# Two attention layers on one core: q and k of a head pair by seven block products, one PSUM tile for the preparation, and a second partial sum of p

## The chip, the core and the metric

The kernel runs on one core of a Trainium2 chip. The core has five instruction queues that run side by side and wait for one another by semaphores: TensorE (PE in the profile; its weight loads are listed apart as PEld), VectorE (DVE), ScalarE (ACT), GpSimd (POOL) and SyncE (SP). Here POOL and SP mostly issue DMA transfers. Each queue works in the order in which its instructions were written. The metric is the device time of one execution in microseconds (us).

## The reference

The input x has 16 images of 256 channels with 32 x 32 = 1024 positions. Two layers of the same form, with weights of their own, are applied to each image. A layer normalises in 16 groups, projects to q, k and v, and attends with 4 heads of 64 channels, where a position term is added to the scores:

```python
q, k, v = proj(Wq, bq), proj(Wk, bk), proj(Wv, bv)      # 256 x 256 times 256 x 1024
sim  = einsum('bhdi,bhdj->bhij', q, k)
rel  = (rel_h + rel_w).reshape(heads, d, n)
qpos = einsum('hdi,bhdj->bhij', rel, q)
attn = softmax(sim + qpos, axis=-1)
out  = einsum('bhdn,bhmn->bhdm', v, attn)
x = x + conv(gn(x))                                     # layer 0, then layer 1
```

Everything is float32. The group normalisation subtracts the mean of a group of columns and divides by its standard deviation.

## The kernel before

**Units, pairs and blocks.** A unit is one image in one layer; there are 32 of them, in an order in which a layer-1 unit stands several units behind its layer-0 unit. A unit has two pairs of heads (`pr`), since two heads of 64 channels fill 128 partitions. A pair has two halves of 512 query columns. A block is one unit, one pair and one half, so a unit has four blocks, b = 0 to 3. Blocks b = 0 and 2 are called even here, b = 1 and 3 odd; n is the number of the block from the start, 0 to 127.

**One block.** It makes eight score tiles j = 0 to 7 of 128 x 1024 (128 keys, two heads, 512 queries). For each, VectorE first writes the position term into a PSUM tile (`seed`, L341), TensorE adds the product of q and k onto it (`scores`, L370), and ScalarE takes exp out of PSUM into a buffer p in SBUF (L391). Then `attend` (L406) multiplies v with the eight p into a PSUM tile po, in two stretches: `values_of_p(0)`, the first score of the next block, then `values_of_p(1)`. ScalarE copies po out (`take_out`, L472). The softmax denominators need the sum of the eight p: `add_up` (L394) adds p 0 to 6 on VectorE, a DMA issued by POOL adds p 7 onto the sum (`add_last`, L432), and further DMAs fold the 128 partitions of that sum together (`fold`, `stack_up`, `fold_again`, `fold_stack`, `spread_sums`), until VectorE takes reciprocals. `finish` multiplies the output by them and adds the residual.

**Matmuls.** Nearly all are 64x64 tiles, four of which run in the array at the same time (two row halves, two column halves). `stretches` (L157) splits work that adds from both row halves into one PSUM bank into two stretches, the second of which waits for the end of the first.

**Preparation.** q, k, v and the position table of the next pair are made in between. `prepare` (L590) gives each block two pieces: b = 0: v of the second key half and q of pair 1; b = 1: k of pair 1 and its positions; b = 2 and 3: the same for pair 0 of the next unit. q and k of a pair (`project`, L255) are each two block products of 128 x 128 weights for each of the two column halves, so eight block products a pair. ScalarE takes each result out in one instruction (L276).

**PSUM.** PSUM holds four tiles of 128 x 1024, tags a to d, that go round in `ring`. In the kernel before, `f0, f1, f2, f3 = ring`; scores go through f0, f1 and f2, but f2 also takes one of the two preparation pieces, and f3 takes the other piece and then po.

**Normalisation.** ScalarE sums, squares and applies it group by group; `norms(u, b, i)` (L624) places these instructions at four places i of a block by tables. The reciprocal root comes from POOL (`rstd`, `nshift`, L234 and L236), between VectorE's reduction of the variance (L232) and ScalarE's applying (L245).

**What sets the order.** The whole fast path is written under a manual schedule: on each engine the instructions stand in the order in which `block` (L637) calls the functions, with nothing moved. The last two blocks of the last unit go through `block_without_pieces`; a general path behind a flag is not run on these inputs.

Of the kernel before, what the change touches and what calls it, by code (L numbers as in the profile page):

```python
# [9 lines left out]
F32 = mybir.dt.float32  # L10
# [7 lines left out]
P = 128  # L18
HALF = 512
G = 16  # L20
# [5 lines left out]
DEN_HI = 1e24  # L26

# [25 lines left out]
def fast_path(ctx, tc, sh, x, layers, out, W, den_all, good, flag):  # L53
# [38 lines left out]
    vpool = ctx.enter_context(tc.tile_pool(name="vpool", bufs=2))  # L92
    ppool = ctx.enter_context(tc.tile_pool(name="ppool", bufs=12))
    apool = ctx.enter_context(tc.tile_pool(name="apool", bufs=3))
# [38 lines left out]

    def taken(parts):
        for l, part in parts:
            w = {"Wq": W.wq, "Wk": W.wk, "Wv": W.wv}[part][l]
            nc.scalar.copy(w.rearrange("p a c -> p (a c)"), raw_t.pop((l, part)))

# [116 lines left out]
    def project(u, pr, which, pk):  # L255

        l = units[u][1]
        w, bias = (W.wk, W.bk) if which == "k" else (W.wq, W.bq)

        def products(t):  # L260
            for cc in range(CC):
                for rs, nh in BANKS[t]:
                    for h, c in enumerate(QUARTERS):
# [3 lines left out]
                            w[l][rs, cc, c0 : c0 + D],  # L267
# [14 lines left out]

    def values(u, g, pv):
        l = units[u][1]
        if g == 0:
            vts[u] = vpool.tile([P, NT, C], F32, tag="v", name=f"v_{u}")
# [17 lines left out]
        def out_of_psum():  # L304
            nc.scalar.copy(
                vts[u][:, 4 * g : 4 * g + 4, :].rearrange("p (a b) c -> p a b c", a=2), pv
            )
# [85 lines left out]

    def add_up(blk, j):  # L394
        u, pr, half = blk
        if j == 0:
            return
        if j == 1:
            accs[blk] = apool.tile([P, 2, HALF], F32, tag="acc", name=f"acc_{u}_{pr}_{half}")
            nc.vector.tensor_tensor(accs[blk], probs[blk, 0], probs[blk, 1], ALU.add)  # L400
        else:
            nc.vector.tensor_tensor(accs[blk], accs[blk], probs[blk, j], ALU.add)  # L402

    QUART = HALF // 2

    def attend(blk, po):  # L406
# [3 lines left out]
        def products(t):  # L410
            for j in range(NT):
                p = probs[blk, j]
                for rs, a in BANKS[t]:
                    for h, c in enumerate(QUARTERS):
# [3 lines left out]
                            vts[u][rs, j, c0 : c0 + D],  # L418
                            p[rs, h, a * QUART : (a + 1) * QUART],
                            start=(t == 0 and j == 0),  # L420
# [11 lines left out]
    def add_last(blk):  # L432
        nc.gpsimd.dma_start(accs[blk], probs[blk, NT - 1], accum_op=ALU.add)  # L433
# [156 lines left out]
    def prepare(u, b):  # L590

        x, y = ring[3], ring[2]
        if b == 0:
            return (
                values(u, 1, psum2(x, f"pv_{u}_1")),
                project(u, 1, "q", psum2(y, f"pq_{u}_1")),
            )
        if b == 1:
            return (
                project(u, 1, "k", psum2(x, f"pk_{u}_1")),  # L600
                positions(u, 1, psum2(y, f"pa_{u}_1")),
            )
        u += 1
        if u == NU:
            return (nothing, nothing), (nothing, nothing)
        if b == 2:
            return (
                project(u, 0, "q", psum2(x, f"pq_{u}_0")),
                project(u, 0, "k", psum2(y, f"pk_{u}_0")),
            )  # L610
        return (
            values(u, 0, psum2(x, f"pv_{u}_0")),
            positions(u, 0, psum2(y, f"pa_{u}_0")),
        )


    APPLY = {0: (0, 1, 5, 9, 9), 1: (9, 9, 9, 11, G)}
    SUMS = {0: (0, 0, 0, 2, 9), 1: (9, 11, 12, G, G)}
    SQUARES = {2: (0, 0, 5, 11, G)}
# [17 lines left out]
    def block(n):  # L637
# [3 lines left out]

        stacked = blocks[n - 3][:2] if half == 1 and n > 2 else None
        summed = blocks[n - 4][:2] if half == 0 and n > 3 else None
        before = blocks[n - 5][:2] if half == 1 and n > 4 else None
        after = blocks[n + 1] if n + 1 < len(blocks) else None
        previous = blocks[n - 1] if n > 0 else None
        one, two = u + 1 < NU, u + 2 < NU

        pieces = u + 1 < NU or b < 2
        if u + 1 == NU and b == 1:  # L650
            widen(u, 1)
        f0, f1, f2, f3 = ring
        folded = n - 1 < FOLDED
        if not pieces:
            return block_without_pieces(n, half)

        if previous:
            if half == 0:
                add_up(previous, 5)
            add_up(previous, 6)  # L660
            if folded:
                add_last(previous)
            else:
                add_up(previous, 7)
        for j in range(1 if n > 0 else 2, 4):
            scores(blk, j)
        (first, first_out), (second, second_out) = prepare(u, b)
        first(0)
        norms(u, b, 0)
        if n == 1:  # L670
            reduced(2, 1)
            added(2)
        seed(blk, 4, f1)
        scores(blk, 4)
        add_up(blk, 1)
        norms(u, b, 1)
        second(0)
        if half == 1:
            second_out()
        if stacked:  # L680
            fold_stack(*stacked, D)
        if summed:
            fold_stack(*summed, R // 8)
            spread_sums(*summed)
        if previous and folded:
            fold(previous)
        if stacked:
            fold_stack(*stacked, R)
        first(1)
        first_out()  # L690
        seed(blk, 5, f0)
        scores(blk, 5)
        if previous and folded:
            stack_up(previous)
# [557 lines left out]
```

## Time and profile before

| | |
|---|---|
| time, median of 3 runs (lowest to highest) | 2531.15 us (2530.21 to 2531.23) |
| profiled execution, first to last instruction (span) | 2528.3 us |
| difference, what lies around the span | 2.85 us against the median |
| busy: VectorE / ScalarE / POOL | 2268.4 / 1948.1 / 815.8 us |
| mean granted TensorE clock | 0.998 |
| DMA queue of POOL (software), share of 16 engines | 31.2% |
| DMA queue of SP (hardware), share of 16 engines | 12.0% |

The profile comes from one execution, and gives its span but no time of its own beyond it; the 2.85 us around it are taken as the same after the change. Matmuls are pipelined and their ends are modelled, so a row of TensorE shows a busy time that overlaps the next row; the distance from one start to the next is what a group takes. In a row of the timeline stand the start and the duration in us, engine, line, operation, tile written and read, and the count of instructions merged. Each float32 matmul shows as two instructions. In brackets stands the idle time before and what ended it.

### The profile page before, as it was taken

Reading aid. Unit: us, or ns where it says so; the run is one execution under the profiler, and the core shown is the slowest. Engines: PE = TensorE matmul, PEld = TensorE weight load, DVE = VectorE, ACT = ScalarE, POOL = GpSimd, SP = SyncE. Lnnn points to the kernel's source line nnn. Section 1 sums busy time; section 2 is a strip of 40 time slices with the busy share of each in tenths; the row PEclk is TensorE's granted clock in tenths of the full one; section 3 lists DMA queues with packets and bytes.
Section 4 is the critical chain, followed back from the end, with each engine's and each line's share of the span. In section 5 each row is a group of like instructions: output and inputs, shape, how many; then the busy total and the mean of one; then the engine's idle time right before and its main releaser. Section 6 shows DMA issues by size and latency. Waiting matters only on the chain.

```text
span 2528.3 us, 85680 instructions
## 1 busy us (share of the span) xinstructions
PE 2507.9 (99%) x37472; PEld 1332.2 (53%) x37472; DVE 2268.4 (90%) x2143; ACT 1948.1 (77%) x3855; POOL 815.8 (32%) x876
## 2 busy tenths in 40 slices
PE   8999999999999999999999999999999999999998
PEld 4555555555555555555555555555555555555554
DVE  7898998999989989999899899998998999989998
ACT  6778777788777787777877778877778777787754
POOL 1332333323333333333233332333333333323320
PEclk9999999999999999999999999999999999999999
DMA  3344444454444444444444444444454444444442
GB/s 94 74 83 80 78 87 77 90 103 88 99 91 101 80 84 95 90 81 98 89 88 96 82 96 80 84 105 91 88 112 81 88 80 84 77 85 80 95 84 67
DMA packets 119838, 221.56 MB, mean 88 GB/s; under 512 B 53912, under 2 KB 55448, under 8 KB 119456
## 3 DMA queue, kind: packets, MB, share of 16 engines
q0 software_dynamic: 53712, 130.10, 31.2%
q1 hardware_dynamic: 65744, 85.90, 12.0%
q8 instruction: 296, 4.85, 0.8%
q14 instruction: 86, 0.70, 0.1%
HBM read 51.78 MB, written 17.30 MB: 27 GB/s over the span
## 4 chain that ended last, share of the span: by engine, by line
PE 96%; DVE 2%; DMA 1%; issue 0%; SPq 0%; ACT 0%; POOL 0%; DVEq 0%; ACTq 0%; POOLq 0%
PE po L416 34%; PE ps L382 34%; PE pv L295 9%; PE pq L265 9%; PE pk L265 8%; PE pa L323 2%; DVE ps L346 1%; DVE acc L402 1%; DMA den_all<-d 0%; PE pm L206 0%; DMA stack<-stack 0%; DMA stack<-acc 0%; DVE acc L400 0%; DMA acc<-p 0%; DMA x<-in_x_dram 0%
## 5 line engine op out<-in xcount | busy, mean ns | idle before, releaser
L346 DVE TENSOR_TENSOR ps<-abt 128x1024 f32<-128x1024 f32 x1018 | 1227.3, 1228 | 228.1 <-ACT p L391 142.9
L391 ACT ACTIVATE p<-ps,shift 128x1024 f32<-128x1024 f32 x1024 | 1092.0, 1115 | 331.8 <-PE ps L382 331.8
L382 PE MATMUL ps<-q,k 64*64 64x512 f32 x8192 | 985.9, 590 | 1.4 <-DVE ps L346 1.2
L416 PE MATMUL po<-p,v 64*64 64x256 f32 x16384 | 930.5, 376 | 0.0
L416 PEld LDWEIGHTS po<-p,v 64*64 64x64 f32 x16384 | 629.4, 133 | 363.4 <-issue 80.9
L402 DVE TENSOR_TENSOR acc<-acc,p 128x1024 f32<-128x1024 f32 x643 | 780.6, 1214 | 7.0
L382 PEld LDWEIGHTS ps<-q,k 64*64 64x64 f32 x8192 | 308.1, 133 | 396.4 <-issue 273.6
L462 POOL DMA_DIRECT2D stack<-stack x310 | 302.3, 975 | 241.9 <-DMA stack<-stack 203.3
L457 POOL DMA_DIRECT2D stack<-acc x248 | 212.9, 982 | 447.3 <-DMA stack<-acc 395.3
L438 POOL DMA_DIRECT2D acc<-acc x124 | 102.8, 829 | 517.1 <-DMA acc<-p 504.4
L433 POOL DMA_DIRECT2D acc<-p x124 | 114.7, 925 | 405.9 <-ACT od L477 254.6
L295 PE MATMUL pv<-Wv,xn 64*64 64x256 f32 x4096 | 244.2, 376 | 0.0
L265 PE MATMUL pk<-xn,Wk 64*64 64x512 f32 x2048 | 242.9, 589 | 0.0
L265 PE MATMUL pq<-xn,Wq 64*64 64x512 f32 x2048 | 242.8, 589 | 0.0
L245 ACT ACTIVATE xn<-x,nshift,rstd 128x128 f32<-128x128 f32 x496 | 211.2, 499 | 0.0
L295 PEld LDWEIGHTS pv<-Wv,xn 64*64 64x64 f32 x4096 | 153.8, 133 | 101.8 <-issue 52.7
L187 ACT ACTIVATE junk<-x,neg 128x128 f32<-128x128 f32 x505 | 197.8, 402 | 0.0
L477 ACT COPY od<-po 128x512 f32<-128x512 f32 x127 | 74.4, 586 | 116.5 <-PE po L416 116.5
L400 DVE TENSOR_TENSOR acc<-p,p 128x1024 f32<-128x1024 f32 x128 | 156.0, 1218 | 0.0
L265 PEld LDWEIGHTS pq<-xn,Wq 64*64 64x64 f32 x2048 | 78.2, 133 | 141.0 <-issue 132.4
L187 ACT ACTIVATE junk<-x 128x128 f32<-128x128 f32 x464 | 141.0, 314 | 0.0
L265 PEld LDWEIGHTS pk<-xn,Wk 64*64 64x64 f32 x2048 | 75.3, 133 | 123.2 <-issue 122.9
(77 smaller groups left out, 1044.8 us busy)
## 6 DMA issues: line engine op xcount, KB each, us to landing
acc<-p POOLq DMA_DIRECT2D x124, 512.0 KB, 5.5
rden<-rd SPq DMA_DIRECT2D x126, 256.0 KB, 6.1
acc<-acc POOLq DMA_DIRECT2D x124, 256.0 KB, 3.5
x<-in_x_dram SPq DMA_DIRECT2D x32, 512.0 KB, 4.0
stack<-acc SPq DMA_DIRECT2D x248, 64.0 KB, 2.1
stack<-acc POOLq DMA_DIRECT2D x248, 64.0 KB, 2.9
out_dram<-x SPq DMA_DIRECT2D x31, 512.0 KB, 3.7
stack<-stack POOLq DMA_DIRECT2D x62, 128.0 KB, 7.1
```

What stands on the lines that cost most here:

```text
L187: nc.scalar.activation(junk, grouped(xt[units[u][0]], g), func, accum_out=into[:, g : g + 1], **bias)
L245: nc.scalar.activation(grouped(xns[u], g), grouped(xt[units[u][0]], g), AF.Identity, bias=shift[:, g : g + 1], scale=rstd[:, g : g + 1],)
L265: yield nc.tensor.matmul(pk[c, nh, :], w[l][rs, cc, c0 : c0 + D], xns[u][rs, cc, nh * HALF : (nh + 1) * HALF], start=(t == 0 and cc == 0), ...
L295: yield nc.tensor.matmul(pv[c, a, i, :], xns[u][rs, cc, j0 : j0 + D], W.wv[l][rs, cc, :], start=(t == 0 and cc == 0 and i == 0), stop=(t = ...
L346: nc.vector.tensor_tensor(ps.rearrange("p h (w y) -> p h w y", y=H), ab[:, :, :H].unsqueeze(2).to_broadcast([P, 2, XH, H]), ab[:, :, H + h ...
L382: nc.tensor.matmul(ps[c, h, :], a[hs, j0 : j0 + D], b[hs, columns], start=bool(tag) and i == 0, stop=i == len(terms) - 1, skip_group_check ...
L391: nc.scalar.activation(p, ps, AF.Exp, bias=W.shift)
L400: nc.vector.tensor_tensor(accs[blk], probs[blk, 0], probs[blk, 1], ALU.add)
L402: nc.vector.tensor_tensor(accs[blk], accs[blk], probs[blk, j], ALU.add)
L416: yield nc.tensor.matmul(po[c, a, :QUART], vts[u][rs, j, c0 : c0 + D], p[rs, h, a * QUART : (a + 1) * QUART], start=(t == 0 and j == 0), s ...
L457: nc.gpsimd.dma_start(at, acc[R:D, h, :], accum_op=ALU.add)
L462: nc.gpsimd.dma_start(stack[:rows_], stack[rows_ : 2 * rows_], accum_op=ALU.add)
```

## The change

**Seven block products.** For a pair, the 2 x 2 block matrix of weights (rows q and k, columns the two channel chunks) meets the 2 x 2 block matrix of the normalised input (rows the chunks, columns the two halves). Before, eight block products are made. Now seven are made from sums and differences of blocks (the scheme of Strassen and Winograd). `forms` builds the sums of weights once per layer, in blocks 1 and 2 of the run; `input_sums` builds the four sums of inputs T1, T3, T2 and T4 on VectorE once per unit, in b = 2 of the unit before. Only the first unit's pairs keep the old way (`project`, called "plain").

```diff
+    def alone(u, pr, ps):
+        f = W.form[units[u][1]]
+        for h, c in enumerate(QUARTERS):
+            c0 = pr * P + h * D
+            nc.tensor.matmul(
+                ps[c, 0, :], f[:, A11, c0 : c0 + D], xb(u, 0, 0),
+                start=True, stop=True, skip_group_check=True,
+            )
+        nc.scalar.copy(ps[:, 1, :], ps[:, 0, :])
+    def two_products(u, pr, step, ps):
+        left, right = (
+            ((S2, A12), (ts[u][:, T2], xb(u, 1, 0))),
+            ((S1, S3), (ts[u][:, T1], ts[u][:, T3])),
+            ((S4, NA22), (xb(u, 1, 1), ts[u][:, T4])),
+        )[step]
...
+    def q_half(u, pr, nh, ps):
+        nc.scalar.activation(
+            qs[u, pr][:, nh * HALF : (nh + 1) * HALF], ps, AF.Identity,
+            bias=W.bq[units[u][1]][:, pr : pr + 1],
+        )
+    def keep(u, pr, nh, ps):
+        nc.scalar.copy(ks[u, pr][:, nh * HALF : (nh + 1) * HALF], ps[:, 0, :])
+    def k_half(u, pr, nh, ps):
+        k = ks[u, pr][:, nh * HALF : (nh + 1) * HALF]
+        nc.vector.scalar_tensor_tensor(
+            k, ps[:, 1, :], W.bk[units[u][1]][:, pr : pr + 1], k, ALU.add, ALU.add,
+        )
```

`alone` is the one product that is made by itself, from 128x64 tiles; ScalarE then copies its result beside it inside PSUM, since it goes into several sums. `two_products` makes two of the other six at a time, in two stretches of 64x64 tiles. Per pair ScalarE has that copy, two `keep` and two `q_half`, each 128 x 512, in place of two instructions of 128 x 1024; VectorE has two `k_half` of 128 x 512.

**Pieces and PSUM.** The ring is now `t0, t1, t2, x`. v, q and k all go through x; scores go through t0, t1 and t2. The even block makes the v piece, the product made alone and the first two products; the odd block makes the other four and the positions (through t0). po of an odd block is in x; po of an even block is in t2, and since t2 may hold anything, ScalarE first sets it to zero (`zeroed`) and `attend` adds onto that.

```diff
-        f0, f1, f2, f3 = ring
+        t0, t1, t2, x = ring
...
+            po = psum2(t2, f"po_{n}")
+                products = two_products(w, pr, 0, qk)
+                products(0)
+            if before:
+                finish(*before)
+            zeroed(po)
+            scores(blk, 7)
...
+            ring[:] = t2, t1, t0, x
```

**Sums of p.** A block of the folded part (all but the last four) now has two sums: `first` = p 0 + p 1 on VectorE plus p 2 by a DMA, and `acc` = p 3 to p 7 on VectorE; a second DMA adds first onto acc (`add_first`) before the fold. VectorE has five additions a block where it had six, POOL two transfers of 512 KB where it had one.

```diff
-        nc.gpsimd.dma_start(accs[blk], probs[blk, NT - 1], accum_op=ALU.add)
+        elif j == 1:
+            firsts[blk] = new_sum(blk, "first", 0, 1)
+            nc.gpsimd.dma_start(firsts[blk], probs[blk, 2], accum_op=ALU.add)
+        elif j == 4:
+            accs[blk] = new_sum(blk, "acc", 3, 4)
...
+        nc.gpsimd.dma_start(accs[blk], firsts.pop(blk), accum_op=ALU.add)
```

**Order and buffers.** `finish` moves from the odd block to the middle of the next even one. The tables of `norms` change: APPLY (b = 0 and 1), SUMS (b = 0 now alone) and SQUARES (b = 2). The buffers of p go from 12 to 9, those of the sums from 3 to 4; v has three buffers of half the size in place of two.

The order on TensorE at the start of the even block n = 58 (unit 14, b = 2), before. In a name the numbers are unit, pair, half and j; pq and pk are q and k of the next unit:

```order
L416 MATMUL po_57_13929<-p_14_0_1_7_13913,v_14_13338 64x256 x4
L382 MATMUL ps_14_1_0_1_13984<-q_14_1_13658,k_14_1_13885 64x512 x4
L382 MATMUL ps_14_1_0_2_13986<-q_14_1_13658,k_14_1_13885 64x512 x4
L382 MATMUL ps_14_1_0_3_13988<-q_14_1_13658,k_14_1_13885 64x512 x4
L265 MATMUL pq_15_0_14050<-xn_15_13510,Wq1_77 64x512 x8
L382 MATMUL ps_14_1_0_4_14060<-q_14_1_13658,k_14_1_13885 64x512 x4
L265 MATMUL pk_15_0_14051<-xn_15_13510,Wk1_79 64x512 x8
L265 MATMUL pq_15_0_14050<-xn_15_13510,Wq1_77 64x512 x8
L382 MATMUL ps_14_1_0_5_14105<-q_14_1_13658,k_14_1_13885 64x512 x4
L265 MATMUL pk_15_0_14051<-xn_15_13510,Wk1_79 64x512 x8
L382 MATMUL ps_14_1_0_6_14127<-q_14_1_13658,k_14_1_13885 64x512 x4
```

And now, with pv the v piece, qk the tile of the seven products and t the sums of inputs (L328 is `alone`, L347 is `two_products`):

```order
L523 MATMUL po_57_14065<-p_14_0_1_7_14022,v_14_1_13693 64x256 x4
L473 MATMUL ps_14_1_0_1_14118<-q_14_1_13769,k_14_1_13770 64x512 x4
L386 MATMUL pv_15_2_14171<-Wv1_79,xn_15_13648 64x256 x16
L473 MATMUL ps_14_1_0_2_14124<-q_14_1_13769,k_14_1_13770 64x512 x4
L386 MATMUL pv_15_2_14171<-Wv1_79,xn_15_13648 64x256 x16
L473 MATMUL ps_14_1_0_3_14127<-q_14_1_13769,k_14_1_13770 64x512 x4
L473 MATMUL ps_14_1_0_4_14203<-q_14_1_13769,k_14_1_13770 64x512 x4
L328 MATMUL qk_15_0_14253<-xn_15_13648,form1_77 64x512 x2
L473 MATMUL ps_14_1_0_5_14235<-q_14_1_13769,k_14_1_13770 64x512 x4
L473 MATMUL ps_14_1_0_6_14259<-q_14_1_13769,k_14_1_13770 64x512 x4
L347 MATMUL qk_15_0_14253<-t_15_14179,form1_77 64x512 x2
```

The v piece now follows the first score of the block, where three scores stood; and score 6 follows score 3 with two scores and the lone product between them.

The same queue at the start of the odd block n = 59, before:

```order
L382 MATMUL ps_14_1_1_1_14201<-q_14_1_13658,k_14_1_13885 64x512 x4
L382 MATMUL ps_14_1_1_2_14203<-q_14_1_13658,k_14_1_13885 64x512 x4
L382 MATMUL ps_14_1_1_3_14205<-q_14_1_13658,k_14_1_13885 64x512 x4
L295 MATMUL pv_15_0_14279<-Wv1_81,xn_15_13510 64x256 x16
L382 MATMUL ps_14_1_1_4_14298<-q_14_1_13658,k_14_1_13885 64x512 x4
L323 MATMUL pa_15_0_14281<-rel1_89,q_15_0_14103 64x64 x32
L295 MATMUL pv_15_0_14279<-Wv1_81,xn_15_13510 64x256 x16
L382 MATMUL ps_14_1_1_5_14363<-q_14_1_13658,k_14_1_13885 64x512 x4
```

And now:

```order
L347 MATMUL qk_15_0_14253<-t_15_14179,form1_77 64x512 x4
L473 MATMUL ps_14_1_1_1_14355<-q_14_1_13769,k_14_1_13770 64x512 x4
L347 MATMUL qk_15_0_14253<-t_15_14179,form1_77 64x512 x4
L473 MATMUL ps_14_1_1_2_14362<-q_14_1_13769,k_14_1_13770 64x512 x4
L473 MATMUL ps_14_1_1_3_14424<-q_14_1_13769,k_14_1_13770 64x512 x4
L473 MATMUL ps_14_1_1_4_14437<-q_14_1_13769,k_14_1_13770 64x512 x4
L347 MATMUL qk_15_0_14253<-xn_15_13648,form1_77 64x512 x2
L347 MATMUL qk_15_0_14253<-t_15_14179,form1_77 64x512 x2
L473 MATMUL ps_14_1_1_5_14456<-q_14_1_13769,k_14_1_13770 64x512 x4
```

Score 4 takes the PSUM tile of score 1, and score 5 that of score 2. In both cases three groups of four matmuls now stand between the one and the other; the position piece has gone behind the block's last score.

The order on ScalarE in the same even block, now:

```order
L584 COPY od_14_0_13936<-po_57_14065 128x512
L482 ACTIVATE p_14_1_0_1_14177<-ps_14_1_0_1_14118,shift_71 128x1024
L208 ACTIVATE junk_16_0_14197,sum_16_14122<-x_9_13166,neg_16_14120 128x128
L208 ACTIVATE junk_16_1_14199,sum_16_14122<-x_9_13166,neg_16_14120 128x128
L208 ACTIVATE junk_16_2_14201,sum_16_14122<-x_9_13166,neg_16_14120 128x128
L482 ACTIVATE p_14_1_0_2_14209<-ps_14_1_0_2_14124,shift_71 128x1024
L396 COPY v_15_0_14172<-pv_15_2_14171 128x1024
L482 ACTIVATE p_14_1_0_3_14241<-ps_14_1_0_3_14127,shift_71 128x1024
L482 ACTIVATE p_14_1_0_4_14251<-ps_14_1_0_4_14203,shift_71 128x1024
L332 COPY qk_15_0_14253<-qk_15_0_14253 128x512
```

Before, exp 1 to 4 of this block stood one behind the other here, with no copy between; the copy of v (L396) now stands ahead of exp 3.

More of the change, by code (lines that the diff above doesn't have):

```diff
@@ L26 @@
 DEN_HI = 1e24
+A11, A12, NA22, S1, S2, S3, S4 = range(7)
+T1, T3, T2, T4 = range(4)
 class Shape:
@@ L640, in block @@
         pr_, half = blk[1:]
[L642 to L649, printed above, removed]
+        even = half == 0
+        last = n == len(blocks) - 3
         if u + 1 == NU and b == 1:
@@ L651, in block @@
             widen(u, 1)
[L652 to L654 removed]
+        if u + 1 == NU and b > 1:
             return block_without_pieces(n, half)
[L657 to L666 removed]
@@ L667, in block @@
[L667 to L694, printed above, removed]
-        add_up(blk, 2)
-        if n == 0:
-            reduced(2, 0)
-        if half == 0:
-            second(1)
-            second_out()
-        seed(blk, 6, f1)
-        scores(blk, 6)
-        if half == 0:
-            ring[2:] = f3, f2
-        seed(blk, 7, ring[2])
-        scores(blk, 7)
@@ L707, in block @@
-        add_up(blk, 3)
-        add_up(blk, 4)
-        if after:
-            seed(after, 0, f0)
+        stacked = blocks[n - 3][:2] if not even and n > 2 else None
+        summed = blocks[n - 4][:2] if even and n > 3 else None
+        before = blocks[n - 6][:2] if even and n > 5 else blocks[n - 5][:2] if last else None
+        after, previous = blocks[n + 1], blocks[n - 1] if n > 0 else None
+        two = u + 2 < NU
+        folded = previous and n - 1 < FOLDED
+        w, pr = (u, 1) if b < 2 else (u + 1, 0)
@@ L752, in block @@
         pos[n] = po
+        if even:
+            if not plain:
+                kept[w, pr] = qk
+        else:
+            ring[:] = t2, t1, t0, x
+    kept = {}
     flatden = den_all.rearrange("p n e -> p (n e)")
```

303 lines of the change are left out of this document (230 added, 73 removed).

## The prediction

> **What bounds the kernel now.** I read the page's busy times first, then the chain of work that ended last.
>
> ```profile
> span 2528.3 us, 85680 instructions
> PE 2507.9 (99%) x37472; PEld 1332.2 (53%) x37472; DVE 2268.4 (90%) x2143; ACT 1948.1 (77%) x3855; POOL 815.8 (32%) x876
> PE 96%; DVE 2%; DMA 1%; issue 0%; SPq 0%; ACT 0%; POOL 0%; DVEq 0%; ACTq 0%; POOLq 0%
> ```
>
> TensorE holds 96% of the chain. Whether its rows are full, only the timeline tells, since ends are modelled. An odd block of the middle, with the block's groups in order:
>
> ```profile
> 1211.94 3.63 PE L416 MATMUL po<-p,v 64*64 64x256 f32 x64
> 1215.40 2.75 PE L382 MATMUL ps<-q,k 64*64 64x512 f32 x24
> 1217.97 1.90 PE L265 MATMUL pk<-xn,Wk 64*64 64x512 f32 x16
> 1219.69 1.04 PE L382 MATMUL ps<-q,k 64*64 64x512 f32 x8
> 1220.55 1.11 PE L323 MATMUL pa<-rel,q 64*64 64x64 f32 x64
> 1221.48 1.90 PE L265 MATMUL pk<-xn,Wk 64*64 64x512 f32 x16
> ```
>
> Start to start, three scores take 2.57 us, so one takes 0.857; a stretch of q or k (16 instructions) 1.72, half of it again 0.86; a stretch of po 3.46; the positions 0.93. Then the busy times by stretch over one unit (the stretches run from po to po; the sum is over four):
>
> ```profile
> core 0: us, PE busy (x) PEld busy (x) DVE busy (x) ACT busy (x) POOL busy (x), PEclk, DMA share, GB/s
> 1207.63:1225.77 18.14, 18.14 (x292) 9.50 (x288) 15.72 (x16) 15.96 (x40) 5.09 (x6) 1.00 0.46 92
> 1264.69:1285.50 20.81, 20.81 (x304) 11.16 (x300) 19.40 (x19) 13.16 (x17) 9.94 (x10) 1.00 0.47 90
> sum 77.87, PE 77.87 PEld 41.28 DVE 70.23 ACT 61.42 POOL 25.63; mean PE 19.47 PEld 10.32 DVE 17.56 ACT 15.35 POOL 6.41
> ```
>
> A unit is 32 scores (27.42), 8 stretches of po (27.68), 4 of v (6.88), 8 of q and k (13.76), two positions (1.86) and small ones (0.16): 77.76 of 77.87 us. **TensorE streams without a gap**; a matmul less is time less, unless the new order makes TensorE wait.
>
> **The saving.** A pair's q and k are four 1.72 stretches, 6.88 us. The seven products are the lone one and six quarter groups, 7 x 0.86 = 6.02, if the two 128x64 matmuls of the lone one run side by side (below). That is 0.86 less for 62 pairs (64 less the first unit's two): 1.72 a unit, 53 us over 31 units.
>
> **What it gives back.** A score tile goes round: VectorE seeds, TensorE adds, ScalarE takes exp, VectorE seeds again. Each link has its row:
>
> ```profile
> 1215.64 0.59 ACT L477 COPY od<-po 128x512 f32<-128x512 f32 x1 [0.26 <-PE po L416]
> 1216.50 3.12 ACT L391 ACTIVATE p<-ps,shift 128x1024 f32<-128x1024 f32 x3 [0.27 <-PE ps L382]
> 1217.65 1.23 DVE L346 TENSOR_TENSOR ps<-abt 128x1024 f32<-128x1024 f32 x1 [1.84 <-ACT p L391]
> 1222.20 2.36 DVE L346 TENSOR_TENSOR ps<-abt 128x1024 f32<-128x1024 f32 x2
> ...
> 20.89 3.49 DVE L346 TENSOR_TENSOR ps<-abt 128x1024 f32<-128x1024 f32 x3
> 22.17 1.09 PE L382 MATMUL ps<-q,k 64*64 64x512 f32 x8 [1.25 <-DVE ps L346]
> 23.08 1.91 PE L295 MATMUL pv<-Wv,xn 64*64 64x256 f32 x32
> ```
>
> Score start to exp start 1.10 (1215.40 to 1216.50); exp 1.115, the next one 1.00 behind it (3.12 for three); exp end to seed start 0.04; a seed 1.23, the next 1.14 behind it. From seed to score there is one clean row: the first of the three seeds ends at 22.12, the score starts at 22.17, and takes 0.91 to the next start in place of 0.857, so 0.11 in all. **The round is 1.10 + 1.115 + 0.04 + 1.23 + 0.11 = 3.59 us.** The other end for that last link:
>
> ```profile
> 1003.01 1.23 DVE L346 TENSOR_TENSOR ps<-abt 128x1024 f32<-128x1024 f32 x1
> 1004.45 1.04 PE L382 MATMUL ps<-q,k 64*64 64x512 f32 x8
> ```
>
> Here 0.21 passed, though TensorE was busy until then anyway, so this is a ceiling: a round of 3.69. I take 0.11, since there TensorE stood idle for that seed alone.
>
> Before, at least 4.3 us of other work lay between two scores of a tile (scores 4 and 6 in the odd block: 0.86 + 0.93 + 1.72 + 0.86). Now:
>
> *Odd block, score 1 to 4 and score 2 to 5:* four groups of 0.857, 3.43. Score 4 comes 0.16 late. That delay also covers score 5, unless ScalarE or VectorE adds to it: in b = 3, `k_half` sits before seed 5 and makes 0.02 more, 0.18; in b = 1 one normalising instruction (0.42, a quarter of the row of 1287.60 below) and `keep` (half of 1.00) sit between exp 1 and exp 2: 1.96 + 1.00 + 0.42 + 0.48 = 3.86 in place of 3.67 us into the block, so 0.34. Sum 0.52 a unit; bounds 0 (no link as long as I read it) and 0.72 (ceiling).
>
> *Even block, score 3 to 6:* also four groups, 3.43, and the copy of v sits ahead of exp 3 on ScalarE:
>
> ```profile
> 25.66 1.91 PE L295 MATMUL pv<-Wv,xn 64*64 64x256 f32 x32
> 27.64 1.01 ACT L305 COPY v<-pv 128x1024 f32<-128x1024 f32 x1 [0.61 <-PE pv L295]
> 28.55 2.13 ACT L391 ACTIVATE p<-ps,shift 128x1024 f32<-128x1024 f32 x2
> 1287.60 1.68 ACT L245 ACTIVATE xn<-x,nshift,rstd 128x128 f32<-128x128 f32 x4
> ```
>
> From the end of v (25.66 + 1.72) to the copy 0.26, to exp 0.91: 1.17 in place of 1.10, so 3.66. That would be 0.23 late. But the lone product is in the way as well, because its tiles have another shape:
>
> ```profile
> 2506.94 3.74 PE L416 MATMUL po<-p,v 64*64 64x256 f32 x64
> 2510.61 1.08 PE L573 MATMUL pd<-acc,ones 128*64 128x512 f32 x4
> 2511.52 1.03 PE L573 MATMUL pd<-p,ones 128*64 128x512 f32 x4
> 2512.48 3.69 PE L416 MATMUL po<-p,v 64*64 64x256 f32 x64
> ```
>
> Four instructions take 0.91 (2510.61 to 2511.52), so two such matmuls do run side by side. But po ended at 2506.94 + 3.46 = 2510.40, and pd starts 0.21 later; pd ended at 2512.38, and po starts 0.10 later. I charge 0.31 for going into the other shape and back: score 6 then follows score 3 by 3.74, the round of 3.66 is covered, and the even block pays 0.31. Bounds: 0.23 (the tail's gaps have another cause; then the round shows) to 0.31. A unit: 0.62.
>
> The Trainium skill's page "TensorEngine Tiling (Array Packing)", section Key Properties, says that changing the tiling mode, not just the tile, drains TensorE. This speaks against the lone product's shape; the trace of before has the shape only at its tail, where the gaps agree with it. Without the rule the even block would cost 0.23, and the forecast would be 5 us lower.
>
> *Even block, v piece:* it is written to x, where po of the odd block was. TensorE has only score 1 (0.857) in between; `take_out` needs 0.24 + 0.59 (row of 1215.64) and 0.11 behind it: 0.94. 0.08 late, 0.16 a unit; bounds 0 and 0.36.
>
> **The other engines.**
>
> ```profile
> L402 DVE TENSOR_TENSOR acc<-acc,p 128x1024 f32<-128x1024 f32 x643 | 780.6, 1214 | 7.0
> L559 DVE SCALAR_TENSOR_TENSOR x<-od,bv,x 128x512 f32<-128x512 f32 x2 | 1.5, 752 | 0.1
> L276 ACT ACTIVATE q<-pq,bq 128x1024 f32<-128x1024 f32 x63 | 70.3, 1115 | 30.5 <-PE pq L265 30.5
> acc<-p POOLq DMA_DIRECT2D x124, 512.0 KB, 5.5
> ```
>
> VectorE, per unit: four additions less, -4.9; four `k_half`, bounded by 0.6 (half an addition) and 0.75 (L559), 2.7 with 0.68; input sums, one of 1.2 and two of 0.6, 2.4. Net +0.2: 70.4 of 77.4 us, 91%. ScalarE: four of 1.115 less, ten halves at 0.59 and two `zeroed` at 0.59 more (their row is nearest; a full 1.1 at worst): +2.6, 64 of 77.4. Neither becomes the bound on the whole; where they sit before a seed is counted above. The moved `finish` (2.4 us of VectorE) falls behind seed 7, and the seed after it is still done some 2 us before its score. POOL: one transfer of 512 KB more a block, 5.5 us to land; `first` is issued half a block before `add_first` needs it, and a sum's buffer is used again some 10 us after its last fold by my count. I charge 0. The p buffers: exp j waits for p j-1 of the block before, read by then: 0.
>
> *Edges:* VectorE's eight `forms` and a second `finish` (2.4) in the last unit's b = 1: +3 us once.
>
> **Sum.** Per unit -1.72 + 0.62 + 0.52 + 0.16 = -0.42, over 31 units -13; with the edges -10. Made against the profiled execution, 2528.3 becomes 2518; with the same 2.85 us around it, **2521 us** against the median of 2531.15.
>
> **Rivals.**
>
> *The rounds are covered (0.17).* If the links are shorter than I read, 0.52 and 0.16 go: -1.10 x 31 + 3 = -31, 2500 us. For it: 0.08 to 0.16 us each is the size of my reading errors. Against it: 3.43 is under every sum of links I can form.
>
> *The waits eat the saving (0.18).* With the ceiling of 3.69 and 0.36 for x: -1.72 + 0.62 + 0.72 + 0.36 = -0.02 a unit, about 2533 with the edges. For it: every small wait for which I charge 0 adds here.
>
> *The normalisation comes late, slower (0.20).* Its place is from b = 3 into b = 0.
>
> ```profile
> 1255.26 0.87 POOL L433 DMA_DIRECT2D acc<-p  x1 [4.43 <-ACT od L477]
> ...
> 1262.44 0.81 POOL L438 DMA_DIRECT2D acc<-acc  x1 [5.45 <-DMA acc<-p]
> ...
> 1269.82 3.79 POOL L234 TENSOR_TENSOR rstd<-var,mhalf 128x16 f32<-128x16 f32 x1
> 1273.69 0.64 POOL L236 TENSOR_TENSOR nshift<-neg,rstd 128x16 f32<-128x16 f32 x1
> ...
> acc<-acc POOLq DMA_DIRECT2D x124, 256.0 KB, 3.5
> ...
> stack<-acc SPq DMA_DIRECT2D x248, 64.0 KB, 2.1
> ```
>
> Before, `rstd` began 1.67 us behind the first po stretch of b = 3 (1264.69 + 3.46 to 1269.82), and the first use stood behind three scores and a stretch of q in b = 0. Now the first use stands behind exp 1: 2.1 us into b = 0, ahead of exp 2, the copy of v and exp 3. On POOL `rstd` stands behind `fold_again`, and that behind a chain that starts with `add_first` 1.2 us into b = 3: 7.2 (1255.26 to 1262.44) to the fold, 3.5 to land, 0.6 + 2.1 for the stack, 1.9 for two issues: 16.5. Then 3.8 + 0.6 for `rstd` and its partner: 20.9, which is 2.4 into b = 0 with a block of 18.5. So by my count 0.3 late; about 1.2 is absorbed before exp 3. From 0.9 us more on, each us costs a us per unit: at one us beyond, 31 more, 2552. For it: one more 512 KB transfer a block shares the queue, and POOL's is in order. Against it: 7.2 is above the median of 5.5.
>
> That the count of matmuls doesn't fall is ruled out by the order: 28 in place of 32 quarter matmuls' time a pair.
>
> **How the numbers follow.** Forecast 0.45, own range 2510 to 2530. 0.2% (5 us) is about what a measurement of this kernel can tell from no change. Faster: 0.9 of the forecast and the first rival, 0.58; same: a tenth of the forecast and most of the second, 0.19; slower: the third and the rest of the second, 0.23. Range 2498 to 2548: from the covered rounds to most of the late normalisation; some 0.15 lies outside.
>
> **What would show it.** One unit in the middle should be 77.4 us of TensorE, odd blocks near 18.5 and even ones near 20.2. Score 4 of odd blocks should start 0.1 behind a seed's end, with TensorE's loads waiting for VectorE there. The lone product should have about 0.2 before and 0.1 after it; if not, the even block is 0.1 shorter. The v piece should wait for the copy of po. If ScalarE waits for `nshift` in b = 0 for over 2 us, the third rival has won; if units come to 76.0, the first one. A wait of VectorE for a DMA before the first addition into `acc` would show that my 10 us of slack are wrong.

## The result, and the profile after

| | before | after |
|---|---|---|
| time, median (lowest to highest) | 2530.89 us (2530.21 to 2531.23), 4 runs | 2560.76 us (2555.67 to 2562.87), 4 runs |
| ratio, 95% interval | | 1.0117 (1.0102 to 1.0131) |
| profiled execution: time, span | span 2528.3 us | 2561.73 us, span 2560.0 us |

The change makes the kernel 30 us slower. The prediction was 2521 us with a range up to 2548: wrong in sign. Span, busy times, the chain of work that ended last, and of the DMA rows the queue of POOL (packets, MB, share of 16 engines) and two kinds of transfer (count, size, median us from issue to landing), after:

```profile
span 2560.0 us, 85203 instructions
PE 2508.2 (98%) x36728; PEld 1281.6 (50%) x36728; DVE 2301.3 (90%) x2244; ACT 2021.6 (79%) x4106; POOL 928.5 (36%) x1000
q0 software_dynamic: 71568, 195.12, 44.6%
PE 45%; DMA 22%; issue 14%; POOL 8%; DVE 7%; SPq 2%; ACT 2%; POOLq 0%; DVEq 0%; ACTq 0%
acc<-first POOLq DMA_DIRECT2D x124, 512.0 KB, 5.7
stack<-acc SPq DMA_DIRECT2D x248, 64.0 KB, 3.5
```

TensorE's busy time has hardly moved (2507.9 to 2508.2), though it has 744 matmul records less: the modelled busy time includes waits. What moved is the chain: before, it ran along TensorE for 96% of the span; now more than half of it runs through transfers, issues, GpSimd and VectorE. And the small transfer that stacks the sums takes 3.5 us to land, where it took 2.1.

The waits (engine, tile and line that waited, what it waited for: us in total, times, longest) and the group of the applying instructions (busy, mean ns of one, idle time before) say where that chain touches the rest:

```profile
PEld ps L473 <- DVE ps L437: 227.8, 395, 2.6
PEld qk L328 <- ACT v L396: 71.6, 62, 3.6
ACT xn L266 <- POOL nshift L257: 62.0, 26, 4.4
PE qk L328 <- ACT v L396: 20.0, 19, 2.7
L266 ACT ACTIVATE xn<-x,nshift,rstd 128x128 f32<-128x128 f32 x496 | 206.7, 496 | 62.0 <-POOL nshift L257 62.0
```

ScalarE waits for `nshift` 26 times, 62.0 us in all; before, this group's idle time was 0.0. The copy of v stands behind it on ScalarE, and the lone product (L328) behind that copy.

The length of each block, from the starts of its po stretches in TensorE's timeline, over the 30 units in between the ends (the stretch from the end of one po to the end of the next):

| | b = 2 | b = 3 | b = 0 | b = 1 |
|---|---|---|---|---|
| before, every unit | 20.64 | 18.28 | 20.66 | 18.26 |
| after | 20.19 | 18.49 | 20.2 in 4 units, 20.4 in 7, 21.5 in 11, 21.9 in 7, 24.5 in 1 | 18.57 |

Three of the four blocks are what the prediction worked out (20.2, 18.5, 18.5), and a unit without lateness (a wait for an input that comes too late) is 77.45 us where 77.4 was forecast. The blocks b = 0 lie 31.5 us above 30 x 20.19 in sum. The two profiled spans differ by 31.7 us: what the other blocks save, and what the two ends of the run cost, nearly cancel.

One late unit, GpSimd and then ScalarE (the block b = 3 runs from 1263.15 to 1281.64):

```profile
1264.53 0.86 POOL L540 DMA_DIRECT2D acc<-first  x1 [4.13 <-DVE acc L502]
...
1272.39 0.81 POOL L545 DMA_DIRECT2D acc<-acc  x1 [6.13 <-DMA acc<-first]
1273.03 0.98 POOL L569 DMA_DIRECT2D stack<-stack  x1
1274.65 0.88 POOL L498 DMA_DIRECT2D first<-p  x1 [0.64 <-ACT p L482]
1278.42 0.79 POOL L569 DMA_DIRECT2D stack<-stack  x1 [2.89 <-DMA stack<-stack]
1281.01 1.72 POOL L564 DMA_DIRECT2D stack<-acc  x2 [1.79 <-issue]
1282.10 4.34 POOL L255 TENSOR_TENSOR rstd<-var,mhalf 128x16 f32<-128x16 f32 x1
1286.52 0.22 POOL L257 TENSOR_TENSOR nshift<-neg,rstd 128x16 f32<-128x16 f32 x1
```

```profile
1282.74 1.11 ACT L482 ACTIVATE p<-ps,shift 128x1024 f32<-128x1024 f32 x1 [0.28 <-PE ps L473]
1286.77 1.27 ACT L266 ACTIVATE xn<-x,nshift,rstd 128x128 f32<-128x128 f32 x3 [2.92 <-POOL nshift L257]
1287.95 1.09 ACT L482 ACTIVATE p<-ps,shift 128x1024 f32<-128x1024 f32 x1
1288.95 0.99 ACT L396 COPY v<-pv 128x1024 f32<-128x1024 f32 x1
```

`rstd` stands behind `fold_again` (L564) and begins 17.6 us after `add_first` (L540). VectorE had `var` ready at 1277.74, 4.4 us earlier. ScalarE wants `nshift` behind exp 1, at about 1283.75, which is 19.2 us after `add_first`; it comes at 1286.74, 22.2 us after.

From the end of `nshift` in 28 units of the middle, counted from the issue of `add_first` (before: of `add_last`), comes the comparison that decides:

| end of nshift, us after | before | after |
|---|---|---|
| up to 19.3 | 13 | 3 |
| 20.3 to 20.7 | 11 | 8 |
| 21.2 to 21.8 | 4 | 11 |
| 22.2 and above | 0 | 6 |
| mean | 19.9 | 21.3 |

Before, the first use stood about 4.1 us into b = 0, 21.4 us after (1276.68, where `add_last` was issued at 1255.26), so none of this cost anything. Now it is wanted at 19.2. Two things came together: the use moved 2.2 us ahead, and the chain became 1.4 us longer in the mean.

The length of the block follows the end of `nshift`, unit by unit: 20.19 up to 19.3, 20.36 at 20.7, 21.47 at 21.8, 21.89 at 22.2 and 24.51 at 23.7; only two units, in which `add_first` itself was late, fall out of this row. Some 1.3 us behind 19.2 cost nothing, and from there on a us costs a us or more. This allows an estimate of what each of the two did alone. With the arrivals of before, only the four units of 21.2 and above would have been late, by about 1 us each: the earlier use alone would have cost some 4 us. With the arrivals of after and the use at 21.4, only one unit would have come more than 1 us late. No run separates the two in this way.

### The profile page after: what moved, and what is told of

Read it like the earlier page. It is cut to its first block, busy times and chain, and to the rows that moved or that the text cites. A ratio compares the mean times of both kernels' runs of the same rounds, so it can differ in the third digit from the quotient of the medians.

```text
span 2560.0 us, 85203 instructions
## 1 busy us (share of the span) xinstructions
PE 2508.2 (98%) x36728; PEld 1281.6 (50%) x36728; DVE 2301.3 (90%) x2244; ACT 2021.6 (79%) x4106; POOL 928.5 (36%) x1000
## 4 chain that ended last, share of the span: by engine, by line
PE 45%; DMA 22%; issue 14%; POOL 8%; DVE 7%; SPq 2%; ACT 2%; POOLq 0%; DVEq 0%; ACTq 0%
PE ps L473 16%; PE po L523 16%; DMA stack<-acc 8%; DMA acc<-acc 7%; PE qk L347 7%; DMA acc<-first 4%; PE pv L386 3%; DVE ps L437 3%; POOL stack L564 3%; DMA stack<-stack 3%; POOL rstd L255 3%; DVE acc L502 2%; SPq L577 2%; PE pa L414 1%; POOL stack L569 1%
## 5 line engine op out<-in xcount | busy, mean ns | idle before, releaser
L482 ACT ACTIVATE p<-ps,shift 128x1024 f32<-128x1024 f32 x1024 | 1108.0, 1114 | 318.0 <-PE ps L473 306.9
L473 PE MATMUL ps<-q,k 64*64 64x512 f32 x8192 | 1032.8, 597 | 11.1 <-DVE ps L437 10.9
L473 PEld LDWEIGHTS ps<-q,k 64*64 64x64 f32 x8192 | 287.9, 133 | 489.7 <-DVE ps L437 227.8
L502 DVE TENSOR_TENSOR acc<-acc,p 128x1024 f32<-128x1024 f32 x372 | 451.4, 1213 | 6.3
L564 POOL DMA_DIRECT2D stack<-acc x248 | 214.6, 946 | 569.3 <-DMA stack<-acc 508.1
L347 PE MATMUL qk<-t,form 64*64 64x512 f32 x1984 | 385.6, 590 | 0.0
L347 PE MATMUL qk<-xn,form 64*64 64x512 f32 x992 | 256.8, 591 | 0.0
L540 POOL DMA_DIRECT2D acc<-first x124 | 122.2, 985 | 231.7 <-DVE acc L502 213.6
L347 PEld LDWEIGHTS qk<-t,form 64*64 64x64 f32 x1984 | 110.3, 133 | 110.4 <-issue 61.5
L498 POOL DMA_DIRECT2D first<-p x124 | 128.2, 1034 | 100.2 <-ACT p L482 92.8
L487 DVE TENSOR_TENSOR first<-p,p 128x1024 f32<-128x1024 f32 x124 | 151.1, 1218 | 0.0
```

The lines of the kernel that those rows point to most:

```text
L347: yield nc.tensor.matmul(ps[c, a, :], f[rs, left[a], c0 : c0 + D], right[a][rs, :], start=(t == 0 and step == 1 and a == 1), stop=(t == 1) ...
L473: nc.tensor.matmul(ps[c, h, :], a[hs, j0 : j0 + D], b[hs, columns], start=bool(tag) and i == 0, stop=i == len(terms) - 1, skip_group_check ...
L482: nc.scalar.activation(p, ps, AF.Exp, bias=W.shift)
L487: nc.vector.tensor_tensor(t, probs[blk, a], probs[blk, b], ALU.add)
L564: nc.gpsimd.dma_start(at, acc[R:D, h, :], accum_op=ALU.add)
```

## The experiments

Each kernel is the changed kernel with the edit shown, unless another base is named. Medians of before in the same job were 2530.13 us (19 runs) for the first four, 2529.86 us (16 runs) for the last three.

**rstd ahead of fold_again** in GpSimd's queue, in odd blocks:

```diff
-        if not even and folded:
-            fold_again(previous)
...
         if two and not even or n == 0:
             mean_out()
+        if not even and folded:
+            fold_again(previous)
```

> Only GpSimd's order changes: in odd blocks fold_again is issued behind rstd and nshift instead of ahead of them. Theory A (the 33 us by which the b = 0 blocks are longer than 20.19 are lateness of rstd, which stands in GpSimd's queue behind the fold chain, issued 16 us after add_first, though VectorE's var is there 13 us after it): rstd starts 1 to 4 us earlier, nshift ends within 19.5 us of add_first, the b = 0 blocks fall from 20.2 to 24.5 to 20.2 to 20.4, and the time falls from 2560.8 to about 2530. Theory B (GpSimd is slow by itself there, because VectorE is busy with two inputs from SBUF; the start of rstd does not matter): rstd grows longer as it starts earlier, the end stays near 21.3 us after add_first, time within 5 us of 2560. Theory C (the lateness is elsewhere: DMA transfers collide): b = 0 stays, time within 5 us.

Measured: 2527.69 us (2526.44 to 2529.73), ratio to before 0.9991 (0.9981 to 1.0). All b = 0 blocks but one (20.38) are 20.19 or 20.20. The same place, GpSimd and then ScalarE:

```profile
1256.50 0.88 POOL L540 DMA_DIRECT2D acc<-first  x1 [4.21 <-DVE acc L502]
...
1262.73 0.81 POOL L545 DMA_DIRECT2D acc<-acc  x1 [4.49 <-DMA acc<-first]
...
1269.80 3.96 POOL L255 TENSOR_TENSOR rstd<-var,mhalf 128x16 f32<-128x16 f32 x1
1273.84 0.64 POOL L257 TENSOR_TENSOR nshift<-neg,rstd 128x16 f32<-128x16 f32 x1
1274.44 1.77 POOL L564 DMA_DIRECT2D stack<-acc  x2
```

```profile
1274.70 1.12 ACT L482 ACTIVATE p<-ps,shift 128x1024 f32<-128x1024 f32 x1 [0.27 <-PE ps L473]
1275.72 1.28 ACT L266 ACTIVATE xn<-x,nshift,rstd 128x128 f32<-128x128 f32 x3
```

`nshift` ends 18.0 us after `add_first` in 25 of the 28 units, whatever the transfers do, and `fold_again`, now behind it, costs nothing. Two calls in another order on a queue that is 36% busy are worth 33 us. Theory A holds; B and C fall.

**The use put off**, GpSimd's order left as it is:

```diff
-    APPLY = {0: (0, 3, 3, 3, 3), 1: (3, 4, 4, 11, G)}
-    SUMS = {0: (0, 0, 0, 9, G)}
+    APPLY = {0: (0, 0, 0, 3, 3), 1: (3, 4, 4, 11, G)}
+    SUMS = {0: (0, 0, 0, 6, G)}
```

> GpSimd and the DMAs stay as they are; the three applying instructions of b = 0 move from behind exp 1 to behind q_half near the end of the block, some 11 us later, and three of the nine sums that stood there go to the next place, beside the second po stretch. Theory A (the lateness of nshift costs only because it is used 2.1 us into b = 0): no wait of ScalarE for nshift is left, every b = 0 block is 20.19, time about 2528, and nshift itself ends as late as before (21.3 us after add_first in the mean). Rival C (the b = 0 blocks are long for another reason, transfers or seeds): b = 0 stays at 20.2 to 24.5, 2560. A cost on the side: three sums more beside the second po stretch may make take_out 0.6 us late, at most 0.2 us in the next block, 6 us in all.

Measured: 2527.26 us (2526.44 to 2528.18), ratio 0.9988 (0.9978 to 0.9998). Every b = 0 block of the 30 units is 20.19 or 20.20. The group of the applying instructions and the chain:

```profile
L266 ACT ACTIVATE xn<-x,nshift,rstd 128x128 f32<-128x128 f32 x496 | 208.4, 501 | 0.0
PE 95%; DVE 3%; issue 1%; ACT 1%; DMA 0%; SPq 0%; DVEq 0%; ACTq 0%
```

`nshift` still ends 21.6 us after `add_first` in the mean, and nobody minds. The cure from the other side gives the same time within 0.5 us: lateness against this one use was the whole loss.

**No 512 KB transfer beside the stacking**, in b = 3 alone:

```diff
-            nc.gpsimd.dma_start(firsts[blk], probs[blk, 2], accum_op=ALU.add)
+            if index[blk] % BPU == 3:
+                nc.vector.tensor_tensor(firsts[blk], firsts[blk], probs[blk, 2], ALU.add)
+            else:
+                nc.gpsimd.dma_start(firsts[blk], probs[blk, 2], accum_op=ALU.add)
```

> In the blocks b = 3 alone, p 2 is added onto first by VectorE instead of by a 512 KB transfer, so that no such transfer is in flight while the sums are stacked. Theory D (the second 512 KB transfer lengthens the fold chain of b = 3, which took 21.3 us from add_first to the end of nshift in the mean where it took 19.9 before): the link from the stacking to fold_again falls from 4.05 to about 2.9 us, nshift ends 20.2 us after add_first in the mean, and of the 33 us of lateness about 25 go: 2536. Rival A alone (the chain is no longer than it was, only the use is earlier): the link stays at 4 us and the time within 5 us of 2560, or 5 to 10 us more for the 1.2 us of VectorE a unit.

Measured: 2542.41 us (2542.22 to 2542.78), ratio 1.0048 (1.0032 to 1.0065). The transfer of the stacking (median over all blocks) and the wait for `nshift`:

```profile
stack<-acc SPq DMA_DIRECT2D x248, 64.0 KB, 2.6
ACT xn L266 <- POOL nshift L257: 12.9, 16, 2.9
```

From the issue of the stacking to that of `fold_again` it takes 3.0 us in the mean of the 28 units, against 4.05 after the change and 2.9 before; `nshift` ends at 19.85, and its spread is that of before again (13 units at 19.1, 14 at 20.4, one at 21.7). In 29 of 30 units b = 0 is 20.2. So theory D holds: the second transfer made the chain longer by delaying a small one beside it; the links before it did not change (from `add_first` to the fold 7.0 us before and after). It is the link that shows it, and not the time: b = 3 became 18.93, so the use of `nshift` also stands 0.43 us later, and hardly any lateness was left where 8 us had been expected. VectorE's addition in b = 3 costs these 0.43 us a unit, 13 us in all, which theory D had left out, and so the time lies 6 us above what D expected.

**The lone product made twice from 64x64 tiles**, in two stretches, one behind score 4 and one behind score 5, with no copy in PSUM:

```diff
-            nc.tensor.matmul(
-                ps[c, 0, :], f[:, A11, c0 : c0 + D], xb(u, 0, 0),
-                start=True, stop=True, skip_group_check=True,
-            )
-        nc.scalar.copy(ps[:, 1, :], ps[:, 0, :])
+            for rs, a in BANKS[t]:
...
+                    ins = nc.tensor.matmul(
+                        ps[c, a, :], f[rs, A11, c0 : c0 + D], xb(u, 0, 0)[rs, :],
+                        start=(t == 0), stop=(t == 1), skip_group_check=True,
+                    )
```

> The lone product is made by 64x64 tiles in two stretches, each 0.86 us, straight into both banks; the 128x64 tiles and ScalarE's copy inside PSUM go. Everything else stays. Theory S (going into the other tile shape and back costs 0.31 us a block): the even block without lateness goes from 20.19 to 20.74 (0.86 more, 0.31 less), 62 blocks, 34 us: 2595. Rival (the shape costs nothing and the 0.31 us were waits for seeds or for the copy): 21.05, 53 us more: 2614. In between, the difference to 21.05 is the cost of the shape. The lateness in b = 0 stays as it is, about 33 us, in both cases.

Measured: 2599.28 us (2589.92 to 2604.62), ratio 1.028 (1.0263 to 1.0297). The even block without lateness is 20.735: 0.545 more, so 0.31 less than a doubled product would add. TensorE's timeline of the changed kernel around the lone product, then of this one:

```profile
1248.20 1.90 PE L473 MATMUL ps<-q,k 64*64 64x512 f32 x16
1250.03 1.08 PE L328 MATMUL qk<-xn,form 128*64 128x512 f32 x4
1251.04 1.95 PE L473 MATMUL ps<-q,k 64*64 64x512 f32 x16
```

```profile
1270.74 1.90 PE L489 MATMUL ps<-q,k 64*64 64x512 f32 x16
1272.45 1.04 PE L333 MATMUL qk<-xn,form 64*64 64x512 f32 x8
1273.31 1.04 PE L489 MATMUL ps<-q,k 64*64 64x512 f32 x8
```

With one shape throughout, two scores take 1.71 from start to start and the product 0.86. With the other shape in between it is 1.83 and 1.01: 0.12 going in, 0.15 coming out, and 0.05 in the scores behind. The rest of the time above before is lateness in b = 0, as large as ever (29 us in the profiled execution of 2589.92 us). The edit also lets the first of the six products wait for the lone one; in the even blocks without lateness TensorE shows no gap there.

**No normalising instruction between exp 1 and exp 2 in b = 1** (base: the use put off):

```diff
-    APPLY = {0: (0, 0, 0, 3, 3), 1: (3, 4, 4, 11, G)}
-    SUMS = {0: (0, 0, 0, 6, G)}
+    APPLY = {0: (0, 0, 0, 4, 4), 1: (4, 4, 4, 11, G)}
+    SUMS = {0: (0, 0, 0, 5, G)}
```

> As the kernel with the late use, and in b = 1 no normalising instruction stands between exp 1 and exp 2 any more: all four of the first groups are applied near the end of b = 0. Theory R (score 5 of b = 1 is late because that instruction, 0.42 us, delays exp 2, and so the seed of score 5): b = 1 falls from 18.58 to the 18.49 of b = 3, 0.09 a unit, about 2.7 us: 2524.5 us where the late use alone gave 2527.3. Rival (b = 1 is longer for another reason, such as the small matmuls of the mean): 18.58 stays, 2527.

Measured: 2524.9 us (2524.05 to 2527.09), ratio 0.9981 (0.9971 to 0.999). b = 1 is 18.49 in every unit: 2.4 us less, as theory R expected.

**Half a seed for scores 4 and 5 of odd blocks** (base: the kernel just above):

```diff
+        nh = 1 if half == 1 and j in (4, 5) else 2
...
-                        start=bool(tag) and i == 0,
+                        start=bool(tag) and i == 0 or not tag and half == 1 and h == 1 and j in (4, 5),
```

> As the kernel before it in this row, with scores 4 and 5 of the odd blocks seeded for one head only; for the other head the product of q and k starts afresh, so its position term is left out in these two tiles. TensorE's work is the same. Theory R (a tile's round through VectorE, TensorE and ScalarE takes 3.59 us where the work between scores 1 and 4, 2 and 5 is 3.43, so TensorE waits): with 0.57 us less of VectorE the round is 3.03, the wait goes, both odd blocks fall from 18.49 to about 18.31, 11 us in all: about 2513. Rival (the odd blocks' 0.18 us above the sum of their matmuls are not the rounds, but drains between stretches or the load of weights): 18.49 stays, within 2 us of the kernel before it.

Measured: 2509.49 us (2509.3 to 2510.18), 15.4 us less; both odd blocks are 18.26, as before the change. This kernel leaves out the position term of one head in two tiles, so it shows what the seeds cost and is no cure. TensorE's timeline of an odd block, its first product, then scores 2 to 4, score 5, and scores 6 and 7, in the kernel above and in this one:

```profile
1176.14 1.04 PE L347 MATMUL qk<-t,form 64*64 64x512 f32 x8
...
1178.71 2.91 PE L473 MATMUL ps<-q,k 64*64 64x512 f32 x24
...
1182.33 1.09 PE L473 MATMUL ps<-q,k 64*64 64x512 f32 x8
...
1184.10 1.90 PE L473 MATMUL ps<-q,k 64*64 64x512 f32 x16
```

```profile
1169.84 1.04 PE L347 MATMUL qk<-t,form 64*64 64x512 f32 x8
...
1172.42 2.75 PE L474 MATMUL ps<-q,k 64*64 64x512 f32 x24
...
1175.85 1.04 PE L474 MATMUL ps<-q,k 64*64 64x512 f32 x8
...
1177.57 1.90 PE L474 MATMUL ps<-q,k 64*64 64x512 f32 x16
```

From score 2 to score 5, three scores and a quarter group, it takes 3.62 with whole seeds and 3.43 with half ones, where 4 x 0.857 is 3.43; another 0.05 goes between scores 5 and 6. The round through the other engines costs 0.24 us in such a block, 0.06 more than I had worked out, and that is why this kernel gained 4 us more than expected.

**The two ends** (base: the kernel with the light b = 1, with `rstd` ahead of `fold_again`; that base was not run, and the numbers are compared with the kernel with the light b = 1, which has no late b = 0 block either). At the start score 2 stands ahead of the v piece, the zeroing of po ahead of the copy of q, and `forms` at the ends of blocks 0 and 1. In the last unit, additions, `widen` and `finish` stand behind the seeds:

```diff
+            if n == 0:
+                scores(blk, 2)
             v(0)
...
             zeroed(po)
+            if plain:
+                q_out()
+                forms(0)
...
+            if n == 1:
+                forms(1)
...
+            if whole:
+                widen(u, 1)
+                add_up(blk, 3)
+                add_up(blk, 4)
             add_up(blk, 5)
             seed(after, 3, t2)
+            if last:
+                finish(*before)
```

> As the first kernel of this row, with rstd ahead of fold_again in GpSimd's queue, and with the work at the two ends moved: at the start score 2 goes ahead of the first v piece, the zeroing of po ahead of the copy of q, and the sums of weights to the ends of blocks 0 and 1 (they stood at the heads of blocks 1 and 2, ahead of seeds); in the last unit the additions of the unfolded blocks, the widening of the position table and the finish go behind the seeds that waited for them. Theory E (the waits of TensorE at the two ends, 1.13, 0.87, 0.24, 1.39 and 0.23 at the start, 1.3 in the first b = 2, and 1.72, 1.70 and 0.74 in the last unit, are these instructions ahead of a seed or copy): 5 to 8.5 us less than the first kernel of this row, 2516 to 2520, below the kernel before the change by 0.4 to 0.55%. Rival (VectorE is full there, and what is moved is late at the next place): less than 2 us gained.

Measured: 2521.65 us (2520.83 to 2522.49), ratio 0.9967 (0.9955 to 0.9979): 0.3% faster than before the change, and the fastest of these kernels that leave nothing out. It is 3.2 us below the kernel with the light b = 1, less than the 5 to 8.5 us that were expected against the kernel with `rstd` first. TensorE's waits at the start in the base, then those at the start and in the last unit in this kernel:

```profile
29.06 1.96 PE L386 MATMUL pv<-Wv,xn 64*64 64x256 f32 x32 [1.13 <-ACT v L396]
42.19 3.68 PE L523 MATMUL po<-p,v 64*64 64x256 f32 x64 [0.87 <-ACT po L508]
...
58.17 3.36 PE L473 MATMUL ps<-q,k 64*64 64x512 f32 x24 [1.39 <-DVE ps L437]
```

```profile
28.86 1.96 PE L386 MATMUL pv<-Wv,xn 64*64 64x256 f32 x32 [0.27 <-ACT v L396]
...
55.37 1.09 PE L473 MATMUL ps<-q,k 64*64 64x512 f32 x8 [0.36 <-DVE ps L437]
56.80 3.36 PE L473 MATMUL ps<-q,k 64*64 64x512 f32 x24 [0.34 <-DVE ps L437]
...
2463.72 1.09 PE L473 MATMUL ps<-q,k 64*64 64x512 f32 x8 [0.31 <-DVE ps L437]
2471.92 1.09 PE L473 MATMUL ps<-q,k 64*64 64x512 f32 x8 [1.93 <-DVE ps L437]
2476.76 1.06 PE L594 MATMUL po<-acc,ones 128*32 128x256 f32 x12 [1.42 <-DVE acc L495]
```

At the start the waits of 1.13, 0.87 and 1.39 us are down to 0.27, none and 0.34; the first unit ends 3.3 us earlier, which is the whole gain. In the last unit theory E fails and the rival holds: three waits of 4.2 us in all became three of 3.7 at other places. VectorE stands ahead of all three, as the rival said.

## Why the prediction was wrong, step by step

- **The saving, 1.72 a unit:** it came. Units without lateness are 77.45 us, 0.38 below before; 0.42 was forecast. With the terms as measured below, the sum is -1.72 + 0.62 + 0.56 + 0.16 = -0.38.
- **The other shape, 0.31 an even block:** right, 0.31 by the doubled product. The split was 0.12 and 0.15 where the tail's rows gave 0.21 and 0.10.
- **The odd rounds, 0.52 a unit:** the mechanism was right and the size 0.04 short: 0.24 in b = 3, and 0.32 in b = 1 (0.08 of it by the normalising instruction).
- **The v piece, 0.16 a unit:** right. It starts 0.89 behind score 1 (1242.95 to 1243.84 in the unit of the late case), 0.03 over the score's own 0.857; and its first stretch takes 1.78 us to the next score where its second takes 1.73, 0.05 more. Together that is 0.08 in each of the two even blocks, and TensorE's loads for v wait 62 times for the copy of po, as told.
- **The ends, +3 us:** too low. With the lateness gone (the use put off), the span is 2525.9 us against 2528.3; 31 units at -0.37 (77.46 there) would make -11.5, so the ends cost about 9. TensorE's ten waits there, 4.8 us in the first unit and 4.2 in the last, make up 9.0; the kernel before has none of them. In the changed kernel itself the ends cost 12, and the further 3 us, in the last unit and behind it, stay unexplained. I priced VectorE's added work, but not which seed it stands ahead of; nor did I look at the copies of v and q ahead of a piece and of the zeroing.
- **"POOL: ... I charge 0": this step failed.** It looked at whether the added transfers' own users would wait. What they did was to delay a small transfer beside them (the stacking, 2.1 to 3.5 us), and this lengthened by 1.4 us a chain behind which `rstd` is queued. By the estimate above, the earlier use would have cost some 4 of the 31.5 us without it.
- **The third rival, 0.20, is what happened,** as told: in b = 3, behind `fold_again`, wanted 2.1 us into b = 0, with ScalarE waiting 2.4 us each time in the mean. Its price was right too: 31.5 us over 30 units is about the one us a unit for which it gave 2552, and with the ends 6 us dearer that is 2558. About 1.2 us of each wait is absorbed, as worked out: (62.0 - 31.5) / 26. Its reason was only near the truth: it had the added transfer share POOL's queue, but the transfers of this chain in that queue changed little (5.5 to 5.7 and 3.5 to 3.8 us), and the one that was delayed goes through SyncE's.
- **What kept it a rival** was the count of "0.3 late". It puts the end of `nshift` at 19.7 us after `add_first`, close to the mean of before, 19.9. What it lacked was the lengthening, charged 0, and the spread: it took several links from one unit, whose `nshift` ended at 19.07, and 15 of 28 units ended 1.3 to 2.4 us later than that. With 1.4 us more, most units passed the 0.9 us from which the rival decides.

The range failed with it: 2548 took in most of the late chain, but not the late chain and the dearer ends together.

## What to carry to other kernels

Before work is moved ahead, look at when its input arrives in every repetition of the loop, not in one: here a steady period on the bound engine hid a spread of 2.4 us behind it. On an in-order queue, short work that someone waits for belongs ahead of steps that wait for transfers, when its own input is there earlier. A new transfer is priced by the small ones beside it, and by what is queued behind those.

## What the hardware showed that was not expected

`rstd` is one instruction of 128x16 elements, and takes 3.9 us in the mean within the blocks. At the start of the kernel, the same operation, beside single-input reductions on VectorE, took 2.9 us. In the units, VectorE's instructions have two inputs from SBUF nearly all the time, and `nshift` ends at a few fixed distances (19.1, 20.4 or 21.5 us before the change) that lie 1.1 to 1.3 us apart, about one such instruction (1.2 us). The two rows of `rstd` in the changed kernel (busy, mean ns):

```profile
L255 POOL TENSOR_TENSOR rstd<-var,mhalf 128x16 f32<-128x16 f32 x31 | 120.1, 3873 | 12.7 <-DVE var L253 12.7
L1080 POOL TENSOR_TENSOR rstd<-var,mhalf 128x16 f32<-128x16 f32 x1 | 2.9, 2938 | 12.5 <-DVE var L1078 12.5
```

The Trainium skill's page "SBUF — State Buffer", section "SBUF: two separate sides", says that VectorE and GpSimd share a pair of ports, which an instruction of VectorE with two SBUF inputs locks against a GpSimd instruction that reads SBUF. These rows agree with it; no run here took VectorE's instructions away, so it isn't shown as the cause.

The times of the kernels with lateness also spread more from run to run: 7.2 us over four runs after the change and 14.7 for the doubled product, against 0.6 to 3.3 us for every kernel without or almost without it. This fits a time that is set by a chain of transfers; it was not tested by itself.
